# Linear attention: the first layer's opening steps moved into the last cycles of the cross attention before it

## The chip, the cores and the metric

One core of a Trainium2 chip runs the whole program in one launch. The metric is the device time of that launch in microseconds (us). The engines named below are TensorE (PE, with its weight loads as PEld), VectorE (DVE), ScalarE (ACT), GpSimd (POOL), and SyncE (SP), whose queue issues most of the DMAs. They run side by side, each through its own list of instructions in order, and wait for each other by semaphores.

## The reference, cut to what matters

The model is a stack of cross attentions, self attentions and feed-forward layers over 16 sequences of 64 tokens with 256 features, so 1024 tokens. Only its first two blocks bear on the change. The first is a cross attention of 16 heads against a context of 1601 rows for each of the 16 sequences, whose output is added to `x`:

```
scores = einsum('bhqd,bhkd->bhqk', qp, kp) / sqrt(d_k)   # masked where exactly 0 in the lower triangle
x = x + concat(softmax(scores) @ vp) @ w_o
```

The second is a linear attention of four layers. Its input is a layer norm of `x` times sqrt(256) with a table of positions added, and each layer begins with a layer norm of its own:

```
y = (x - mean) / sqrt(var + 1e-5) * sqrt(D) + pos        # once, the input of layer 0
h = (y - mean) / sqrt(var + 1e-5) * ln1_s + ln1_b        # each layer
q, k, v = h @ Wq + bq, h @ Wk + bk, h @ Wv + bv          # elu(q)+1, elu(k)+1 follow
y = y + (linear attention of q, k, v) @ Wo + bo
y = y + relu(norm(y) @ W1 + b1) @ W2 + b2
```

After the four layers a final norm of `y`, scaled by `lnf_s` and shifted by `lnf_b`, is added to `x`, and a mixture of experts follows.

## The kernel before, in words

Tokens lie on the 128 partitions in eight tiles of 128 (`self.x[:, t]`, two sequences each), all in float32.

The cross attention (`l0_xattn`, L201) is a stream over 16 sequences of 13 context chunks of 128 rows. `stream` (L341) writes its order out by hand for PE: each cycle makes the scores of two chunks by matmuls into one PSUM tile of four banks (`sc`, one buffer), ACT takes their exponential (`e`, L327, three buffers), PE multiplies `e` with the values (`acc`), and POOL adds `e` into the running sums of the softmax (`tot`, L2385). For the last sequence POOL sums only the chunks below 7; PE does the others in `add_sums` (L2285). In the last cycles, where there is nothing left to project, `out(t)` (L336) multiplies token tile t's heads with `wo` and DVE adds the result to `x` (L358). At the end `finish(xs[B - 1])` runs `finish_heads` (L2293): the last sums on PE, then on DVE a reciprocal (`rec`), two products (`half`) and their sum into `xT`, and then `out(7)` makes the last token tile. PE's instructions are pinned to the order of the text (`self.mm`, `self.tr`); those of DVE, ACT and POOL here are put in order by a scheduler.

The linear attention (`l0_attn`, L414) works on two halves of four token tiles, `a` and `b`, with its tiles in a pool on the other side of the memory (`l0a`). Tiles there lie over tiles of the cross attention, and an instruction that first writes one waits for the last reader of what lay below. Before the first layer, `measure` (statistics by bn_stats and bn_aggr, a square root on ACT), `start` (subtract the mean on ACT, multiply and add the positions on DVE) and `norm` (subtract and multiply on DVE) are done for both pairs of tiles of half `a` and the first pair of `b`; the second pair of `b` follows inside the projections of `a`. All of this stands behind the cross attention. `project` (L538) is a generator: `turn` transposes two token tiles on PE and evacuates them with the norm's scale and shift, `kv(t)` projects keys and values of a token tile and DVE evacuates them, `exp_keys` and `larger` make elu+1 of the keys on ACT and DVE, and the queries follow feature by feature. `go(pr, n)` runs n steps of it. In this function V, A and G are DVE, ACT and POOL pinned to the order of the text.

`self.row` (L96) loads a row of biases and spreads it over the partitions. `row_L_attn_bk.0` (L101) holds layer 0's bk, bv, bo and b2, of which DVE needs the first two to evacuate keys and values.

Of the kernel before, what the change touches and what calls it, by code (L numbers as in the profile page):

```python
# [12 lines left out]
F32 = mybir.dt.float32  # L13
I32 = mybir.dt.int32
BF16 = mybir.dt.bfloat16
AF = mybir.ActivationFunctionType
ALU = mybir.AluOpType
# [3 lines left out]
P = 128  # L21
# [43 lines left out]
class Sections:  # L65
# [135 lines left out]
    def l0_xattn(self):  # L201
        nc, tc, d = self.nc, self.tc, self.d

        self.held = ExitStack()
        self.routed = self.held.enter_context(tc.tile_pool(name="l0r", bufs=1, reuse_waits="tile"))
        with ExitStack() as ctx:
            sb = ctx.enter_context(tc.tile_pool(name="l0x", bufs=1, reuse_waits="tile"))
            sb2 = ctx.enter_context(tc.tile_pool(name="l0x2", bufs=2, reuse_waits="tile"))
# [119 lines left out]
                return e  # L328

            def finish(x):  # L330
                self.finish_heads(sb2, hT, x.b, x.acc, self.sums_of(x), ones)

            def extra(x):
                return [(maxima, x, g, i) for g in range(2) for i in range(3)] + [(last_maxima, x), (max_rows, x)]
# [1 line left out]
            def out(t):  # L336
                pm = ps.tile([P, D], F32, tag="bk", name="lin", padded_shape=[P, 512])
                for k in range(KC):
                    self.mm(pm, hT[:, k, t * P : (t + 1) * P], wo[:, k, :], start=(k == 0), stop=(k == KC - 1))
                self.add_to_x(t, pm)  # L340

            self.stream(ps, sb2, load, wk, wv, copy, weights, finish, out, extra)

# [70 lines left out]
    def l0_attn(self):  # L414
# [5 lines left out]
        for name, shape, dt in (("logits", [P, NT, E], F32), ("count", [P, NT + 1, E], F32), ("wt", [P, NT, 2], F32), ("hot", [P, NT, 2, E], F32),  # L420
# [8 lines left out]

        self.taken = tc.dram_tile([E * CAP + 2 * T, D], F32, name="taken")  # L430
        self.given = tc.dram_tile([E * CAP, D], F32, name="given")
        zero = pool.tile([P, D], F32, tag="zero", name="zero")
        nc.gpsimd.memset(zero, 0.0)
        nc.sync.dma_start(
            self.taken[: E * CAP].rearrange("(j p) d -> p j d", p=P), zero.unsqueeze(1).to_broadcast([P, E * CAP // P, D]))
        nc.gpsimd.memset(to.count[:, 0], 0.0)
        views = dram_disjoint_views(self.taken, 2 * NT)
        with ExitStack() as ctx:
# [10 lines left out]

            mask = self.c("mask136")  # L450
            pos = self.c("pos")
            lnf = self.row(sb, "L0_attn_lnf_s", "L0_attn_lnf_b")

            class Half:

# [21 lines left out]
                A.activation(r, r, AF.Sqrt)  # L477
                s.by[p] = mv, r

            def norm(s, src, p):  # L480

                mv, r = s.by[p]
                V.reciprocal(r, r)
                for j in range(2):
                    t = 2 * p + j
                    V.tensor_scalar(s.n[:, t, :], src[:, t, :], mv[:, j, 0:1], r[:, j : j + 1], ALU.subtract, ALU.mult)
# [15 lines left out]
            def add_row(s, r):  # L502
                G.tensor_tensor(s.y, s.y, r.unsqueeze(1).to_broadcast([P, HT, D]), ALU.add)
# [11 lines left out]
                    self.mm(pm, xT[:, k, t * P : (t + 1) * P], w[:, k, :], start=(k == 0), stop=(k == kc - 1))  # L515
                return pm

            def weights(l):
                w = lambda: None
                w.wq = self.w2(d["L0_attn_Wq"][l], "wq")  # L520
                w.wkv = self.wp.tile([P, KC, 2 * D], F32, tag="w8", name="wkv", bufs=3, padded_shape=[P, KC, 1024])
                for j, k in enumerate(("L0_attn_Wk", "L0_attn_Wv")):
                    nc.sync.dma_start(w.wkv[:, :, j * D : (j + 1) * D], d[k][l].rearrange("(c p) n -> p c n", p=P))
                w.wo = self.w2(d["L0_attn_Wo"][l], "wo")
                w.w1 = self.w8(d["L0_attn_W1"][l], "w1")
                w.w2 = self.w8(d["L0_attn_W2"][l], "w2")
                rows = self.row(sb2, *(f"L0_attn_{k}.{l}" for k in ("bk", "bv", "bo", "b2")))
                w.bk, w.bv, w.bo, w.b2 = (rows[:, i * D : (i + 1) * D] for i in range(4))
                for k in ("bq", "b1", "ln1_s", "ln1_b", "ln2_s", "ln2_b"):
                    setattr(w, k, self.v(f"L0_attn_{k}.{l}"))  # L530

                w.bq1 = sb2.tile([P, KC], F32, tag="bq1", name="bq1")
                w.bk1 = sb2.tile([P, D], F32, tag="bk1", name="bk1")
                for out, of in ((w.bq1, w.bq), (w.bk1, w.bk)):
                    G.tensor_scalar(out, of, 1.0, 0.0, ALU.add, ALU.add)
                return w

            def project(s, w):  # L538

                def kv(t):
                    pm = by_token(w.wkv, t, s.hT)
                    V.tensor_tensor(s.kz[:, t, :], pm[:, 0:D], w.bk1, ALU.add)
                    V.tensor_tensor(
                        s.va[:, t, :, 0:128], pm[:, D : 2 * D].rearrange("p (g x) -> p g x", g=2),
                        w.bv.rearrange("p (g x) -> p g x", g=2), ALU.add)

                def two(t):
                    return (a[:, t : t + 2, :].rearrange("p t x -> p (t x)") for a in (s.kz, s.tmp))  # L550

                def exp_keys(t):
                    z, e = two(t)
                    A.activation(e, z, AF.Exp, bias=less)

                def larger(z, e):
                    V.scalar_tensor_tensor(z, e, 1.0, z, ALU.min, ALU.max)

                qe = [s.h1T[:, c, :] for c in range(KC)]
                turn(s, 0, w.ln1_s, w.ln1_b)  # L560
                yield
                for t in range(2):
                    kv(t)
                    yield
                turn(s, 1, w.ln1_s, w.ln1_b)
                add_row(s, w.bo)
                exp_keys(0)
                yield
                for c in range(KC):
                    pm = by_feature(w.wq, c, s.hT)  # L570
                    A.activation(qe[c], pm, AF.Exp, bias=w.bq[:, c : c + 1])
                    A.activation(s.qT[:, c, :], pm, AF.Identity, bias=w.bq1[:, c : c + 1])
                    larger(*(two(0) if c == 0 else (s.qT[:, 0, :], qe[0])))
                    yield
                kv(2)
                larger(s.qT[:, 1, :], qe[1])
                yield
                kv(3)
                yield
                exp_keys(2)  # L580
                larger(*two(2))

            def attend(s, w):

# [96 lines left out]

            def start(s, p):

                mv, r = s.by[p]
                less = sb.tile([P, 2], F32, tag=f"less{s.i}", name="less", bufs=2)
                V.tensor_scalar(less, mv[:, :, 0], -1.0, 0.0, ALU.mult, ALU.add)
                V.reciprocal(r, r)
                V.tensor_scalar(r, r, math.sqrt(D), 0.0, ALU.mult, ALU.add)
                for j in range(2):
                    t = 2 * p + j  # L690
                    A.activation(s.n[:, t, :], s.x[:, t, :], AF.Identity, bias=less[:, j : j + 1])
                    V.scalar_tensor_tensor(s.y[:, t, :], s.n[:, t, :], r[:, j : j + 1], pos, ALU.mult, ALU.add)

            def mix(at, fd):

# [95 lines left out]
            nc.gpsimd.memset(less, -1.0)  # L791
            self.pinned = True
            a, b = Half(0), Half(1)

            a.make("h1T")
            b.make("h1T", "tmp")
            a.make("tmp", "hT", "kz", "va", "qT")
            b.make("n", "kz", "va", "hT", "qT", "y")
            a.make("y", "n")
            w = weights(0)  # L800

            V.pinned = False
            for s, n in ((a, 2), (b, 1)):
                for p in range(n):
                    measure(s, s.x, p)
            for s, n in ((a, 2), (b, 1)):
                for p in range(n):
                    start(s, p)
                    measure(s, s.y, p)
                for p in range(n):  # L810
                    norm(s, s.y, p)
            V.pinned = True
            for s in (a, b):
                nc.gpsimd.memset(s.va[:, :, :, 128:136], 1.0)
            pr = project(a, w)
            go(pr, 3)
            measure(b, b.x, 1)
            go(pr, 1)
            start(b, 1)
            measure(b, b.y, 1)  # L820
            go(pr, 1)
            norm(b, b.y, 1)
            go(pr)
            for s in (a, b):
                G.tensor_tensor(s.x, s.x, lnf[:, D:].unsqueeze(1).to_broadcast([P, HT, D]), ALU.add)
            at, pr = attend(a, w), project(b, w)
            go(pr, 4)
            for _ in range(4):
# [4 lines left out]
            at, fd = attend(b, w), feed(a, w)  # L833
            go(fd, 2)
            mix(at, fd)
            for l in range(1, 4):
                w0, w = w, weights(l)
                for s, ws, o, wo in ((a, w, b, w0), (b, w, a, w)):
# [27 lines left out]
            go(route(b, 1))  # L866
            squares(999)
            self.pinned = False

    def weighted_experts(self, ps, sb2, xT, comb, n, hidden, down):  # L870

# [1418 lines left out]
                    acc[32 * j : 32 * j + 32, 2 + g, :], self.c("ones")[:w, :32], weights[g][j], start=False, stop=True,  # L2290
                    skip_group_check=True)

    def finish_heads(self, sb2, hT, b, acc, totals, ones, eps=None):  # L2293


        nc = self.nc
        self.add_sums(acc, totals, P)
        rec = sb2.tile([P, 2, P], F32, tag="rec", name="rec")
        if eps is None:
            nc.vector.reciprocal(rec, acc[:, 2:4, :])  # L2300
# [21 lines left out]
    def scores_by_key(self, pm, pair, stop):  # L2322
# [3 lines left out]
        for h, (x, c) in enumerate(pair):  # L2326
            i = min(c // 4, 2)
            a = (c - 4 * i) * P
            for g in range(2):
                for r in range(4):  # L2330
# [3 lines left out]
                        x.qb[o, g].rearrange("p h s -> p (h s)"),  # L2334
                        start=(h == 0 and g == 0), stop=stop, skip_group_check=True,
                    )

    def sums_of(self, x):
        return [[x.tot[:, j, 2 * g : 2 * g + 2, :].rearrange("p h s -> p (h s)") for j in range(4)] for g in range(2)]
# [481 lines left out]
```

## Time and profile before

| | us |
|---|---|
| median of 3 runs (3752.28 to 3766.32) | 3760.18 |
| the profiled execution | 3753.96 |
| its span in the profile | 3752.2 |
| PE busy in the span | 3440.3 (92%) |
| DVE, ACT, POOL busy | 1974.1, 1451.3, 1291.0 |
| 850 to 860 us: PE, DVE, ACT busy | 10.00, 2.40, 5.04 |
| 860 to 870 us: PE, DVE, ACT busy | 1.75, 8.70, 2.00 |
| 870 to 880 us: PE, DVE, ACT busy | 1.38, 9.32, 1.61 |
| 880 to 890 us: PE, DVE, ACT busy | 7.46, 3.79, 2.05 |
| 890 to 900 us: PE, DVE, ACT busy | 5.19, 6.73, 7.22 |

The profile is one execution on the chip. A line of the timeline gives the start in us, the duration in us, the engine, the line of the kernel, the operation, what it writes and reads, its shape, how many instructions were merged, and in brackets how long the engine sat idle before it and who ended that. A line of the chain of waits gives start, duration and what held the end of the program up at that time. Where a helper class issues the instruction, its line is L59 (V, A and G), and for pinned matmuls and transposes it is L2452 and L2457. The cross attention ends at about 860 us of the span, the linear attention at about 1359 us.

### The profile page before, as it was taken

The numbers are of one execution on the slowest core, as the hardware profiler recorded it, in microseconds if no ns is written. First come the engines' busy times: TensorE is split into PE (matmuls) and PEld (weight loads), VectorE is DVE, ScalarE is ACT, GpSimd is POOL, SyncE is SP. The second block draws the span as 40 slices with busy tenths as digits, with TensorE's granted clock in tenths as the row PEclk, the third lists the DMA queues.
The fourth block names the chain that finished last, engine by engine and source line by source line (L and its number), as shares of the span: only waits on it lengthen the run. The fifth ranks groups of instructions, "written<-read, shape, count | busy, mean of one in ns | idle before, by whom it ended". The sixth has DMA issues, their size and how long they took to land.

```text
span 3752.2 us, 70803 instructions
## 1 busy us (share of the span) xinstructions
PE 3440.3 (92%) x30966; PEld 2187.8 (58%) x30966; DVE 1974.1 (53%) x3676; ACT 1451.3 (39%) x2076; POOL 1291.0 (34%) x787
## 2 busy tenths in 40 slices
PE   8999999996999969999977988999999789999986
PEld 4555555563665645555545666667767555555554
DVE  5344333436555546656657554577767665333346
ACT  2333333333444414444423443466666612111213
POOL 1555555562011123333321001577777630000012
PEclk9999999998999979999989999999999989999997
DMA  4111001101332344343101001111111004111640
GB/s 145 38 38 38 31 27 38 38 10 35 105 96 87 111 158 163 127 146 110 37 26 40 1 6 44 68 56 38 56 38 38 11 2 174 43 36 30 278 180 13
DMA packets 106123, 258.66 MB, mean 69 GB/s; under 512 B 9203, under 2 KB 74483, under 8 KB 103510
## 3 DMA queue, kind: packets, MB, share of 16 engines
q1 hardware_dynamic: 97366, 222.68, 16.6%
q10 hardware_dynamic: 6912, 27.27, 2.3%
q8 instruction: 243, 3.98, 0.4%
q0 software_dynamic: 1536, 4.20, 0.4%
q14 instruction: 66, 0.54, 0.0%
HBM read 248.34 MB, written 5.77 MB: 68 GB/s over the span
## 4 chain that ended last, share of the span: by engine, by line
PE 77%; DVE 12%; ACT 7%; issue 2%; DMA 1%; POOL 1%; SPq 0%; ACTq 0%; DVEq 0%; POOLq 0%
PE sc L2452 15%; PE pk L2452 15%; PE lin L2452 7%; PE acc L2452 6%; PE lin_t L2452 5%; ACT e L327 5%; PE pu L2452 4%; PE lin L194 3%; PE gate L2017 3%; PE up L2017 3%; PE pc L1639 3%; PE prz L2452 2%; PE gelu_t L1549 2%; PE turn L2457 2%; PE pa L2452 1%
## 5 line engine op out<-in xcount | busy, mean ns | idle before, releaser
L2385 POOL TENSOR_TENSOR tot<-tot,e 128x1024 f32<-128x1024 f32 (+1 forms) x340 | 802.9, 2361 | 374.5 <-ACT e L327 251.2
L270 DVE TENSOR_REDUCE m<-sc 128x4 f32<-128x2048 f32 x96 | 220.1, 2293 | 271.3 <-PE sc L2452 270.2
L1779 DVE SCALAR_TENSOR_TENSOR e<-sc,row_L_xattn_nbias,free 128x2048 f32<-128x2048 f32 x104 | 244.3, 2349 | 121.8 <-PE sc L2452 116.3
L1781 ACT ACTIVATE e<-e 128x2048 f32<-128x2048 f32 x104 | 198.7, 1910 | 243.2 <-DVE e L1779 243.2
L327 ACT ACTIVATE e<-sc 128x2048 f32<-128x2048 f32 x104 | 195.2, 1877 | 241.2 <-PE sc L2452 239.6
L2452 PE MATMUL sc<-qb,kT 32*128 32x128 f32 x6656 | 244.8, 283 | 36.6 <-DVE m L284 12.3
L2452 PEld LDWEIGHTS sc<-qb,kT 32*128 32x128 f32 x6656 | 205.9, 187 | 80.6 <-issue 24.5
L2452 PE MATMUL acc<-e,v 128*32 128x128 f32 x6656 | 226.6, 276 | 6.4 <-ACT e L1782 6.4
L2452 PEld LDWEIGHTS acc<-e,v 128*32 128x32 f32 x6656 | 170.3, 110 | 105.7 <-issue 95.1
L2452 PE MATMUL pk<-cT,wk 128*128 128x512 f32 (+1 forms) x512 | 207.0, 534 | 3.6 <-DVE rows L300 3.6
L2452 PE MATMUL pk<-wv,cT 128*128 128x256 f32 x832 | 209.8, 394 | 0.0
L1782 ACT ACTIVATE e<-e 128x2048 f32<-128x2048 f32 x104 | 198.7, 1911 | 3.3
L2452 PE MATMUL pk<-cT,wkv 128*128 128x512 f32 (+1 forms) x512 | 197.2, 526 | 0.0
L2452 PE MATMUL pk<-wkv,cT 128*128 128x256 f32 x832 | 196.3, 386 | 0.0
L2452 PEld LDWEIGHTS pk<-wv,cT 128*128 128x128 f32 x832 | 149.7, 190 | 75.5 <-issue 58.2
L2452 PEld LDWEIGHTS pk<-wkv,cT 128*128 128x128 f32 x832 | 153.3, 190 | 28.3 <-issue 4.3
L1639 PE MATMUL pc<-ew,eh 128*128 128x256 f32 x640 | 158.8, 391 | 0.0
L2452 PE MATMUL pu<-cn,e 128*64 128x257 f32 (+1 forms) x1248 | 146.5, 391 | 12.9 <-POOL e L1186 12.9
L2452 PE MATMUL sc<-kT,qb 32*128 32x512 f32 (+2 forms) x1536 | 140.8, 465 | 14.9 <-DVE m L270 2.3
L2021 ACT ACTIVATE g<-gate 128x512 f32<-128x512 f32 x68 | 40.6, 597 | 292.2 <-PE gate L2017 292.2
L1176 POOL TENSOR_TENSOR e<-e,mx 128x512 f32<-128x512 f32 x96 | 81.8, 883 | 194.7 <-DVE mx L1175 194.7
L2022 DVE TENSOR_TENSOR hT<-up,g 128x512 f32<-128x512 f32 x68 | 47.0, 692 | 178.8 <-PE up L2017 174.6
(519 smaller groups left out, 6339.5 us busy)
## 6 DMA issues: line engine op xcount, KB each, us to landing
cT<-in_ctx_t SPq DMA_DIRECT2D x128, 832.0 KB, 6.1
cn<-in_ctx_n SPq DMA_DIRECT2D x32, 1664.0 KB, 12.6
piece<-in_ctx_n ACTq DMA_DIRECT2D x32, 640.0 KB, 3.9
w<-in_L_attn_W SPq DMA_DIRECT2D x8, 1024.0 KB, 7.2
piece<-in_ctx_n ACTq DMA_DIRECT2D x16, 384.0 KB, 3.5
w<-in_L_ffn_W SPq DMA_DIRECT2D x16, 256.0 KB, 4.8
down<-in_L_ffn_w_down SPq DMA_DIRECT2D x16, 256.0 KB, 2.7
gate<-in_L_ffn_w_gate SPq DMA_DIRECT2D x16, 256.0 KB, 2.7
```

The source lines that it names most:

```text
L194: nc.tensor.matmul(pm, xT[:, k, t * P : (t + 1) * P], w[:, k, :], start=(k == 0), stop=(k == kc - 1))
L270: nc.vector.tensor_reduce(x.m4[:, g, :, i], pm, AX.X, ALU.max)
L327: nc.scalar.activation(e, pm, AF.Exp, scale=0.25)
L1176: pin(nc.gpsimd.tensor_tensor(p.e, p.e, p.mx.unsqueeze(2).to_broadcast(p.shape), ALU.subtract))
L1549: nc.tensor.matmul(pm, w[:, c, lo : lo + m], cT[:, c, :], start=(c == 0), stop=(c == nk - 1))
L1639: nc.tensor.matmul(pc[:, n, j, :], s.eh[i][:, c, tok], ew2[:, c, cols], start=False, stop=(c == 3))
L1779: nc.vector.scalar_tensor_tensor(e16, pm16, nb, free[:, at : at + P].unsqueeze(1).to_broadcast([P, 16, P]), ALU.add, ALU.mult)
L1781: nc.scalar.activation(e, e, AF.Relu)
L1782: nc.scalar.activation(e, e, AF.Square)
L2017: nc.tensor.matmul(pm[-1], w[:, k, n * P : (n + 1) * P], xT[:, k, tok], start=(k == 0), stop=(k == KC - 1))
L2385: nc.gpsimd.tensor_tensor(tot[:w], x.first if c == 1 else tot[:w], e[:w], ALU.add)
L2452: ins = self.nc.tensor.matmul(*args, **kw)
```

## The change

In `l0_xattn` a new pool `l0y` is opened below the cross attention's own pools and kept to the end of `l0_attn`. It holds half `a`'s `y` and `hT`, and small tiles for the statistics. `out(t)` now also measures the token tile, takes roots after tiles 3, 5 and 7, and for half `a` makes `y` (after tiles 4 and 5) and its norm (after 5 and 6); the transposes of half `a` stand inside the last `finish_heads`, between the last sums on PE and the reciprocal on DVE. Roots there are made as exp(-ln(v)/2) on ACT with one Newton step on DVE.

```
+        self.begun = self.begin(self.at_once.enter_context(tc.tile_pool(name="l0y", bufs=1, reuse_waits="tile")))
...
+                self.finish_heads(sb2, hT, x.b, x.acc, self.sums_of(x), ones, between=turned if x.b == B - 1 else None)
...
+            def start(t):
+                if t == 0:
+                    nx.n = sb2.tile([P, KC, SKP], F32, tag="cT", name="n")[:, 0, : 4 * D].rearrange("p (t d) -> p t d", d=D)
+                nc.scalar.activation(nx.n[:, t], self.x[:, t, :], AF.Identity, bias=nx.less[:, t : t + 1])
+                nc.vector.scalar_tensor_tensor(nx.y[:, t, :], nx.n[:, t], nx.r[:, t : t + 1], pos, ALU.mult, ALU.add)
+                nx.measure(nx.y[:, t, :], nx.mvy[:, t])
+            def norm(p):
+                two = slice(2 * p, 2 * p + 2)
+                nx.root(nx.ry[:, two], nx.mvy[:, two], 1.0)
+                for t in range(2 * p, 2 * p + 2):
+                    nc.vector.tensor_scalar(
+                        nx.n[:, t], nx.y[:, t, :], nx.mvy[:, t, 0:1], nx.ry[:, t : t + 1], ALU.subtract, ALU.mult)
+            def turned():
+                for p in range(2):
+                    pt = ps.tile([P, KC, 2, P], F32, tag="bk", name="tr")
...
+                            self.tr(pt[:, c, j, :], nx.n[:, 2 * p + j, c * P : (c + 1) * P], self.ident)
+                    for c in range(KC):
+                        nc.scalar.activation(
+                            nx.hT[:, c, 2 * p * P : (2 * p + 2) * P], pt[:, c].rearrange("p j x -> p (j x)"), AF.Identity,
+                            bias=ln_b[:, c : c + 1], scale=ln_s[:, c : c + 1])
...
                 self.add_to_x(t, pm)
+                nx.measure(self.x[:, t, :], nx.mv[:, t])
+                if t in (3, 5, 7):
+                    nx.roots(0 if t == 3 else t - 1, t + 1)
+                if t in (4, 5):
+                    start(2 * (t - 4))
+                    start(2 * (t - 4) + 1)
+                if t in (5, 6):
+                    norm(t - 5)
...
+        def root(r, mv, scale, V=nc.vector, A=nc.scalar):
+            vq = pool.tile([P, 2, 4], F32, tag="vq", name="vq")
+            v, q = vq[:, 0, : r.shape[1]], vq[:, 1, : r.shape[1]]
+            V.tensor_scalar(v, mv[:, :, 1], 1e-5, 1.0 / scale**2, ALU.add, ALU.mult)
+            A.activation(q, v, AF.Ln)
+            A.activation(r, q, AF.Exp, scale=-0.5)
+            V.tensor_tensor(q, r, r, ALU.mult)
+            V.scalar_tensor_tensor(q, v, -0.5, q, ALU.mult, ALU.mult)
+            V.scalar_tensor_tensor(r, q, 1.5, r, ALU.add, ALU.mult)
+        def roots(lo, hi):
+            root(nx.r[:, lo:hi], nx.mv[:, lo:hi], math.sqrt(D))
+            nc.vector.tensor_scalar(nx.less[:, lo:hi], nx.mv[:, lo:hi, 0], -1.0, 0.0, ALU.mult, ALU.add)
```

In `l0_attn` the projections of `a` start from the finished `hT` (`project(a, w, True)` skips both `turn`s and puts `add_row` at its end), and both pairs of `b` are prepared between their steps, with roots by `root` on V and A. The row of biases of layer 0 is loaded into `l0a` early in the order of its tiles, and the addition of `lnf_b` to `x` is put behind the first mix of attention and feed-forward. The tile of zeros that clears `taken` in memory is half as wide and is written by two DMAs:

```
-            a.make("h1T")
-            b.make("h1T", "tmp")
...
+            a.y, a.hT = nx.y, nx.hT
+            a.make("n", "tmp", "qT")
+            b.make("y")
+            rows0 = weights_rows(0)
+            a.make("kz", "va")
+            b.make("n", "hT")
+            a.make("h1T")
+            lnf = self.row(sb, "L0_attn_lnf_s", "L0_attn_lnf_b")
+            b.make("tmp", "kz", "va", "qT", "h1T")
+            w = weights(0, rows0)
...
-            pr = project(a, w)
-            go(pr, 3)
-            measure(b, b.x, 1)
-            go(pr, 1)
-            start(b, 1)
...
+            pr = project(a, w, True)
+            go(pr, 1)
+            start(b, 0)
+            go(pr, 2)
+            norm(b, b.y, 0, True)
+            start(b, 1)
+            go(pr, 2)
+            norm(b, b.y, 1, True)
             go(pr)
-            for s in (a, b):
-                G.tensor_tensor(s.x, s.x, lnf[:, D:].unsqueeze(1).to_broadcast([P, HT, D]), ALU.add)
...
-        zero = pool.tile([P, D], F32, tag="zero", name="zero")
+        zero = pool.tile([P, P], F32, tag="zero", name="zero")
...
+        for k in range(KC):
+            nc.sync.dma_start(
+                self.taken[: E * CAP, k * P : (k + 1) * P].rearrange("(j p) d -> p j d", p=P),
+                zero.unsqueeze(1).to_broadcast([P, E * CAP // P, P]))
```

## The prediction

> **What bounds the kernel now.** First the page's shares: PE is busy 92% of the span and the chain that ended last lies on PE for 77%. So only a stretch where PE stands idle can give time. The busy time by 10 us shows one at the seam between the cross attention and the linear attention: PE is busy 10.00 of 10 until 860, then 1.75, 1.38, 7.46 and 5.19. There I read the chain of waits:
>
> ```profile
> 856.35 4.12 PE acc L2452 x144
> 860.48 1.77 DVE rec L2300
> ...
> 863.26 1.35 PE lin L2452 x4
> 864.64 0.42 DVE x L358
> ...
> 873.59 2.87 DVE y L59 x2
> ...
> 880.40 5.75 PE lin L2452 x8
> ...
> 891.73 3.07 DVE y L59 x2
> ...
> 898.95 3.80 PE lin L2452 x4
> ...
> 905.27 5.26 PE lin L2452 x8
> ```
>
> From 860.46 to 880.40 the end waits for DVE: the last heads, then statistics, roots, `y` and `n` of three pairs of tiles. A second, smaller hole lies inside the projections of half a (the second pair of b, 891.7 to 898.95). The `lin` at 880.40 is a's first kv, the one at 905.27 is b's; they are 24.87 apart. I call their starts R and Q. After Q the work is the same, so the change's gain is the move of Q, less what it costs elsewhere.
>
> Two things in the timeline decide how early the moved work can run. DVE and POOL:
>
> ```profile
> 841.36 12.16 POOL L2385 TENSOR_TENSOR tot<-tot,e 128x1024 f32<-128x1024 f32 x5
> ...
> 848.76 2.45 DVE L2311 TENSOR_TENSOR xT<-half 128x128 f32<-128x128 f32 x1
> ...
> 855.41 1.88 ACT L327 ACTIVATE e<-sc 128x2048 f32<-128x2048 f32 x1 [2.38 <-PE sc L2452]
> ...
> 862.92 0.29 DVE L2311 TENSOR_TENSOR xT<-half 128x128 f32<-128x128 f32 x1
> ...
> 877.38 1.31 DVE L59 TENSOR_SCALAR ln_r<-ln_mv 128x2 f32<-128x2 f32 x1
> ```
>
> The same sum into xT takes 0.29 when POOL is still and 2.45 while POOL adds; a tiny scalar step takes 1.31 (0.17 elsewhere) until POOL's addition ends. DVE steps that read PSUM (x at 841.40, 0.42) and bn_stats (0.74 for two beside POOL) do not stretch. So until POOL's last sum at 853.5 each root step on DVE waits up to 2.43. And ACT:
>
> ```profile
> 2093.53 1.06 ACT L1649 ACTIVATE sp<-sp 128x1024 f32<-128x1024 f32 x1
> 2094.49 0.58 ACT L1643 ACTIVATE g<-pc 128x512 f32<-128x512 f32 x1
> 2095.09 1.28 ACT L1650 ACT_TABLE_LOAD   x1
> 2096.38 1.06 ACT L1650 ACTIVATE sp<-sp 128x1024 f32<-128x1024 f32 x1
> ```
>
> This is another block, the only one with ln: L1649 is an exp, L1650 a ln. All 12 ln of the trace come with a table load of 1.28, though the set before them served exp. No row has an exp straight after a ln; bounds 0 and 1.28. I take 1.28, since whoever placed these loads never chose a set that would serve both. So a root costs 2 loads and 2 steps of 0.20: 2.96 on ACT. The root by sqrt that it replaces also costs a load there and one back (892.11, 896.33).
>
> The Trainium skill ("ScalarE: Activation LUTs", Table sets: the hidden batching unit) says that ln followed by exp needs one load, since one set has both. By that rule the later roots would be free of loads and, by the steps below, the time some 7 us lower. The 12 rows speak against it.
>
> **Step 1: a's norm in the tail.** x3 is added at 844.85 and ready at 845.27. Measure: 0.39 + 0.18, so 845.85. The first root (tiles 0 to 3): its scalar step waits for POOL's addition until 846.2; ln and exp with their loads fill ACT from the end of `e` (845.73) to 848.7. The next `e` could start at 847.70, so it is late by 1.0. Three DVE steps and `less` (0.7 by themselves) wait at 851.1 and 853.5 for POOL: ready near 854. Bounds: 850 (no waiting), 856 (a wait at every step). Then four subtractions on ACT (0.45 each), on DVE four y and measures (4 x (0.44 + 0.57) = 4.0) and tiles 4 to 6 added and measured (3 x 0.99 = 3.0): DVE is done with y near 861. It also has rec, half and xT, 2.7 from 860.5 on.
>
> On ACT three more roots are due (tiles 4 and 5, the two pairs of y): 3 x 2.96 = 8.9. The last `e` ends at 857.3, with the delay 858.3. If all come after it, they end at 867; if the lns are batched or run before it, at 861. I take 865 for the last n. To it: n 0.73 (872.86), transposes 0.66 (8 of 16; the others are earlier), and `out(7)`, which PE's pinned order puts between transposes and kv: 1.35. ACT evacuates hT beside it (2 x 0.56). **R becomes 869** with the tail's delay of about 1; range 864 to 876.
>
> The other conditions for R: wkv was issued at 19.85, long before. layer 0's row of biases was issued at 864.67, when out(7) had read xT below it, and POOL had it at 868.72. In the new order of tiles it comes, by their sizes, over the values of sequence 14, whose last matmul is at 837.85; even at the old time it lands before the first evacuation, R + 3.9. `bk1` on POOL (1.09) now waits for out(7), also ready in time.
>
> **Step 2: from R to Q.** Pinned order, in us after R. kv0 reaches its evacuation after 3.9 (880.40 to 884.29, clock granted 0.77 there); evacuation 0.76: 4.7. b's first pair: y 0.89, measures 1.2, scalar step 0.2, ln 0.2, load 1.28, exp 0.2, three steps 0.65: 9.4. The root of tiles 6 and 7 (2.96 on ACT, after out(7)) fits before it. kv1's evacuation 0.76, n 0.73: 10.9. The second pair likewise, 4.6: 15.5; DVE then does `larger` 0.69. ACT frees the queries' first PSUM buffer at 16.4 (exp and identity, 0.57 each in a row), which kv(3) waits for, because `mm` has three; after 4 us idle it takes 3.8 as at 898.95: 20.2. Evacuation 0.76, exp_keys 0.72, larger 0.69, hT 0.46: 22.9. b's `add_row` on POOL (2.34) starts when n has been read and holds `larger` up by 1.4: **Q is R + 24.3**, against 24.87 now. Two y stalls of over 2 us go (POOL's x additions at 876.15 and 892.17 are gone from here), two roots behind kv's evacuation come in their place.
>
> **Sum.** Q: 869 + 24.3 = 893.3 against 905.27, so -12.0.
>
> **Edits at nothing.** (a) The lnf_b additions, 2 x 2.5 on POOL, fall in the first mix, where PE is busy 10.00 of 10 (940 to 960) and POOL idle; DVE, 3.79 to 4.57 of 10, may wait 2.5 once or twice, three PSUM buffers of 1.9 cover that: 0 to +2. (b) The zeros in two DMAs: SP issued the one at 13.17, one more issue is 0.38. The DMA engines are full until 35, while the chain is DVE's gate biases until 33.33 and the next DMA is issued at 55.55; all of it twice is 1280 KB at 370 GB/s = 3.5: 0, bounds 0 and +3.5. (c) Seven measures in the tail, 0.57 each: DVE is busy 0.85 to 4.46 of 10 there. (d) lnf_s is loaded later, needed at 1290. (e) The 16 transposes, 0.15 to 0.17 each, run beside rec (1.77), where PE stood idle: 0; if n is late, they are in R already. (f) POOL's sums wait for DVE's short steps: 5 x 0.2 = 1, in the delay above.
>
> **The rivals.** *More is gained:* lns batched, or one set for both; R at 864, two loads fewer before Q, kv0 at full clock (0.43 for 0.86, 8 matmuls less 2): -19, between -17 and -22. For it: the scheduler can pair waiting lns. Against: the 12 loads. *Half is given back:* the roots queue one after the other behind the last `e` and POOL's waits come at every step: R at 875, -6. *The work does not move ahead:* now every DVE step of this kind stands behind the last xT (863.13); if the list puts the new ones there too, six steps of y and roots follow it as now: R near 880, 0. Against: they are in the same function now, and x was ready from 834.9. *Slower:* ACT runs in order. If ln or the subtractions are listed ahead of `e` at 851.14 and 855.41, `e` waits for DVE, which waits for POOL: each up to 2.45 + 2 x 1.28 = 5.0, PE's end 10 later, at 870.5, then the roots of 8.9, n, transposes and out(7): R at 882.5 and Q at 906.8, +1.5; with (a) and (b) above at their upper ends +7. It decides from R = 881 on. For it: PE has nothing else to do between `sc` and `e` but one `acc` and `lin`; against: `e` stands first in the text and ACT is idle for 1.57 to 2.38 before each.
>
> **How the numbers follow.** The profiled execution took 3753.96 (span 3752.2), 6.2 below the median 3760.18 of the runs shown. -12.0 gives 3742 for such a one and 3748 against the median, which I forecast. Chances: forecast (-8 to -16) 0.53, more 0.19, half 0.14, not ahead 0.06, slower 0.08. 0.5% is 18.8, about what a measurement of this kernel can tell from no change. Faster by more: nearly all of "more" that passes it, 0.15, and 0.02 from the runs' own spread of 14. Slower by more: only if the slower case's stalls come to more than twice their price, or by something that I have not seen: 0.05. Within: 0.78. The range takes -22 of the faster case to the edge of "not ahead" and +2: 3738 to 3762.
>
> **What would show it.** Right: `rec` within 2 us of 860.5; the first `lin` of attention near 869; two table loads at each root; transposes and hT's evacuation beside `rec`; no y of 3 us; Q near 893; the rest moved by the same amount. Wrong: table loads missing; an `e` that waits for DVE or ACT for over 2 us; R after 876; an interval from R to Q above 28; a difference after Q, in the mix or at the experts, of over 3 us.

## The result, and the profile after

The changed kernel takes 3759.37 us, the kernel before on the same chip 3755.47 (medians of 13 runs each). The ratio, which is estimated from all the runs and is not the quotient of the two medians, is 1.0001, with a 95% interval from 0.9991 to 1.0010: no measurable difference, where 12 us less were forecast. The profiled execution took 3760.83 (span 3758.7).

To see where the time went I matched each instruction of DVE, ACT and POOL with its counterpart in the kernel before and took the difference of their starts. It is +1.8 by 80 us and stays so until 838; from 920 to 1340 it is a constant -3.5. So the seam gained 5.3, not 12. Behind it the difference rises to +6.6: by 0.9 between 1350 and 1375, by 5.1 near 1412 and by 5.5 between 3058 and 3080, the rest in smaller steps. The two large steps are not the seam's: e4 below, which has nothing of the work at the seam, has 4.5 and 5.6 at the same places. Below, "net" means less the difference at 765, ahead of the seam.

The chain of waits through the seam (start, duration, what):

```profile
850.98 1.87 DVE vq L2407
...
853.11 2.16 DVE vq L2408
...
855.86 1.58 DVE y L344 x4
...
860.96 1.28 ACT L2406
862.26 0.20 ACT r L2406
862.48 1.28 ACT L2405
...
863.99 1.28 ACT L2406
...
868.90 0.20 ACT ry L2406
869.11 1.77 ACT e L329
870.92 4.54 PE acc L2532 x80
875.49 1.77 DVE rec L2348
...
878.37 1.11 PE lin L2532 x4
```

Before, this stretch was PE's last sums, `rec` at 860.48 and then 20 us of DVE. Now the chain runs over table loads on ACT, and it still has to pass the last `e`. ACT's own rows in the timeline show what stands ahead of it:

```profile
852.05 1.85 ACT L329 ACTIVATE e<-sc 128x2048 f32<-128x2048 f32 x1
856.58 1.88 ACT L329 ACTIVATE e<-sc 128x2048 f32<-128x2048 f32 x1 [2.67 <-PE sc L2532]
858.47 1.28 ACT L2405 ACT_TABLE_LOAD   x1
860.74 0.20 ACT L2405 ACTIVATE vq<-vq 128x2 f32<-128x2 f32 x1 [0.98 <-DVE vq L2404]
...
867.61 1.28 ACT L2406 ACT_TABLE_LOAD   x1
868.90 0.20 ACT L2406 ACTIVATE ry<-vq 128x2 f32<-128x2 f32 x1
869.01 1.86 ACT L329 ACTIVATE e<-sc 128x2048 f32<-128x2048 f32 x1
```

The scores of that last `e` were complete at 862.66:

```profile
862.27 0.39 PE L2532 MATMUL sc<-rows,minus 32*128 32x512 bf16 x4
```

ACT takes its work in order, and three roots with six loads were listed ahead of it; two of the three waited for DVE as well (0.98 ahead of the ln at 860.74, 0.60 ahead of the one at 867.39). So `e` starts 6.35 late. The `e` at 852.05 is late too, by 2.7, behind the first root's exp load and the subtractions. PE waits, and the clock falls (window, its length, busy time of PE, PEld, DVE, ACT, POOL, then the granted clock):

```profile
860.00:870.00 10.00, 5.61 (x144) 4.41 (x136) 4.34 (x22) 8.53 (x12) 1.57 (x5) 0.98 0.01 2
870.00:880.00 10.00, 8.03 (x94) 6.56 (x95) 4.53 (x11) 4.09 (x6) 2.36 (x1) 0.66 0.36 128
```

From `rec` on the change does what it was to do: the transposes and the evacuation of hT run beside it, and a's first kv product starts 3.8 behind it (19.9 before). It starts at R = 879.30, b's at Q = 901.91: net 2.9 and 5.2 earlier than before.

Then the experts. The queue of SP in the kernel before:

```profile
1331.71 0.41 SPq L101 DMA_DIRECT2D row_L_ffn_b<-in_rows  x1
1332.22 12.29 SPq L914 DMA_DIRECT2D w<-in_L_ffn_W  x8
```

and after the change:

```profile
1328.23 0.34 SPq L101 DMA_DIRECT2D row_L_ffn_b<-in_rows  x1
1348.21 4.11 SPq L960 DMA_DIRECT2D w<-in_L_ffn_W  x8
```

Eight weight loads of 256 KB, whose tiles the diff does not touch, go out 20 us later behind the row of biases, just as ACT's last step on a `piece` of the context (1348.00, 0.19) ends. From 1350 to 1360 the DMA engines are then busy 0.93 and 0.75 of each 5 us (0.00 and 0.22 before), and the scatter into `taken`, which everything waits for there, takes longer (before, then after):

```profile
1358.90 2.39 DMA taken<-n,put
```

```profile
1355.40 4.37 DMA taken<-n,put
```

### The profile page after: what moved, and what is told of

It is laid out like the page before. It is cut to its first block, busy times and chain, and to the rows that moved or that the text cites. A ratio compares the mean times of both kernels' runs of the same rounds, so it can differ in the third digit from the quotient of the medians.

```text
span 3758.7 us, 70806 instructions
## 1 busy us (share of the span) xinstructions
PE 3441.4 (92%) x30951; PEld 2185.7 (58%) x30966; DVE 1971.7 (52%) x3681; ACT 1466.3 (39%) x2094; POOL 1292.2 (34%) x787
## 4 chain that ended last, share of the span: by engine, by line
PE 76%; DVE 13%; ACT 8%; issue 2%; DMA 1%; POOL 0%; another core or an unknown queue 0%; SPq 0%; ACTq 0%; DVEq 0%; POOLq 0%
PE sc L2532 15%; PE pk L2532 15%; PE lin L2532 6%; PE acc L2532 6%; PE lin_t L2532 5%; ACT e L329 5%; PE pu L2532 4%; PE lin L194 3%; PE gate L2063 3%; PE up L2063 3%; PE pc L1685 3%; PE prz L2532 2%; PE gelu_t L1595 2%; PE turn L2537 2%; PE pn L2532 1%
## 5 line engine op out<-in xcount | busy, mean ns | idle before, releaser
L2532 PE MATMUL sc<-cT,qT 128*64 128x512 f32 (+1 forms) x768 | 141.9, 522 | 3.8 <-ACT scs L1202 3.3
```

The lines of the kernel that those rows point to most:

```text
L2532: ins = self.nc.tensor.matmul(*args, **kw)
```

## The experiments

Theory: the gain at the seam is eaten because ACT's roots, with their loads, are listed ahead of `e`; the later loss is the late weight loads. Rivals: POOL's sums, which hold DVE's small steps; the loads as such, wherever they stand; the clock's accidents. Q is given net (905.27 before, 900.1 after the change).

**e1_dve_roots**: no root on ACT. In `root`:

```diff
-A.activation(q, v, AF.Ln)
-A.activation(r, q, AF.Exp, scale=-0.5)
+near = D if scale == 1.0 else 1.0 / D
+V.tensor_scalar(r, v, -0.5 * near**-1.5, 1.5 * near**-0.5, ALU.mult, ALU.add)
+for _ in range(2 if scale == 1.0 else 3):
     V.tensor_tensor(q, r, r, ALU.mult)
...
```

The loop holds the three lines of the Newton step. The variance of y is near 256 by construction; that of x is near 1 in these data, and this root of x holds only near there.

> The changed kernel with every root of the new pool taken by VectorE alone: a tangent at the nominal variance (256 of y, 1 of x) and two or three steps of Newton instead of Ln, Exp and one step. No table load and no root on ScalarE is left in the tail, all else is as in the changed kernel. Theory (ScalarE works in order, and the roots with their loads are listed ahead of e): the last e starts within 2 us of 860 instead of 869.0, rec near 864 instead of 875.5, a's first kv product (R) at 867 to 870 instead of 879.3, b's (Q) at 889 to 892 instead of 901.9; 9 to 12 us less than the changed kernel, 0.997 of it. Rival (VectorE's small steps wait for POOL's sums, and so y and the roots are late whoever takes them): the last e is early too, but n is ready as late as now, R stays at 876 or later, and no more than 3 us are gained.

The three last `e` start at 848.78, 852.48 and 856.46, each within 0.4 of the end of its scores. Q = 892.6, a gain of 12.7 instead of 5.2. The time is 0.9984 of before (0.9975 to 0.9993). So the roots on ACT, their loads and their place in the order together, cost 7.5 of the gain. R (873.30) was later than expected, and `rec` came at 868.62 although PE's last sum ended at 863.0: DVE is the bound now. Its column, the third after the window's length:

```profile
850.00:860.00 10.00, 8.32 (x205) 6.39 (x198) 9.68 (x24) 4.39 (x3) 4.30 (x2) 1.00 0.01 2
860.00:870.00 10.00, 5.07 (x120) 3.91 (x111) 8.98 (x42) 1.79 (x4) 3.77 (x6) 0.79 0.38 133
```

**e2_e_first**: the loads stay, the order changes.

```diff
-if t in (3, 5, 7): nx.roots(0 if t == 3 else t - 1, t + 1)
+if t in (3, 7):    nx.roots(t - 3, t + 1)
-if t in (5, 6):    norm(t - 5)
 def turned():
+    nc.vector.tensor_scalar(eps, nx.e[:, 3, 511:512], 0.0, 1e-5, ALU.mult, ALU.add)
+    norm(0, eps)
+    norm(1, eps)
...
```

> The changed kernel with the two roots of a's norm put behind the last e: their 1e-5 comes out of a VectorE step that reads the last e, and the root of tiles 4 and 5 is taken together with that of 6 and 7. Ln, Exp and their table loads remain (two fewer loads). Theory (the order on ScalarE is what costs): the last e starts near 860, rec near 864, the two roots take 2 x 3.5 us behind the last e, so n at 869 and R at 872 to 874; 5 to 8 us less than the changed kernel. Rival (the loads cost wherever they stand, the order does not matter): R within 2 us of 879.3, and no gain.

The rows of ACT:

```profile
860.31 1.88 ACT L329 ACTIVATE e<-sc 128x2048 f32<-128x2048 f32 x1 [2.73 <-PE sc L2536]
862.21 1.28 ACT L2409 ACT_TABLE_LOAD   x1
...
868.45 1.00 ACT L367 ACTIVATE hT<-tr,vecs 128x256 f32<-128x256 f32 x2
```

The last `e` waits for PE alone, R = 874.53 (expected 872 to 874), Q = 896.3; 0.9979 of before (0.9967 to 0.9991). Q is 3.9 earlier than in the changed kernel. One root with its two loads is gone too, 3.0 on ACT, so the order by itself is worth between 0.9 and 3.9; the rival that the order does not matter (R within 2 us of 879.3) falls. `rec` was later than expected (869.8): DVE's root steps stand ahead of it.

**e3_short_pool**: `if x.b < B - 1 or c < 7` becomes `c < 3` for POOL's sums.

> The changed kernel with POOL's sums of the last sequence cut from seven chunks to three; TensorE adds the other four as it adds the last six now. So VectorE's small steps in the tail do not wait for POOL. Ln, Exp, their loads and their place among the e remain. Theory (the order on ScalarE): the last e still stands behind the roots and their loads, R at 876 or later. Rival (POOL's sums hold VectorE, and so the roots, back): the y's start 4 to 6 us earlier, the last e as well, R at 872 to 874.

R = 877.32, and the last `e` at 867.03 still stands behind six loads. Q = 897.9, 2.3 earlier than the changed kernel's. Both effects exist; the roots on ACT are the greater one (7.5 in e1), as the theory had it. One run, 3757.86.

**e4_zero_only**: the kernel before with the two transfers of zeros.

> The kernel before with one edit of the change alone: the zeros go out in two transfers of half a row, from a tile half as wide. If these two transfers cause the 1.8 us that the changed kernel is behind at 78, this kernel is behind by 1.5 to 2.0 there too, and the granted clock falls to 0.50 near 71. If that step comes from the clock alone, which can fall at the same place in any run, the start is within 0.6 us of the kernel before up to 838, or is behind by another amount.

0.3 behind from 80 to 838 (3755.13, one run). The granted clock did fall for one stretch near 68, and still the start was not 1.8 late: in this run the transfers did not bring that step.

**e5_right** and **e6_dve_right**: `tile_pool(name="l0y", bufs=1, side="right")` in the changed kernel and in e1.

> The changed kernel with its new pool laid at the other end of SBUF, where the pool of the linear attention lies too, and nothing else. Theory (the eight weight loads of the expert layer write where y and hT of half a still lie, and so wait for the end of the linear attention): their issue falls from 1348.2 to within 2 us of the row of L0_ffn_b2, near 1328; the scatter into taken then takes near 2.4 us instead of 4.5 and 1.5 to 3.5 us of the changed kernel's time go. The seam itself stays as it is, R near 879. Rival (that loss comes from where the clock's windows fall): the loads move or not, and the time stays within 1 us.

> e1_dve_roots with the new pool at the other end of SBUF. Theory: the two gains add up, since they lie in two places: R near 873, weight loads issued near 1320, and 8 to 11 us less than the kernel before (0.997 to 0.9978 of it). Rival (what the seam gains is given back at the expert layer whatever the loads do, by a wait on something that is not moved): no more than the 6 us that e1_dve_roots gained.

The theory of *where* the loads collide failed: they are issued at 1344.6, 20 us behind the row as before, and the scatter takes 4.68. So it is not a's y and hT that they wait for. Q = 899.8 and 892.6, as without the edit. 0.9989 (0.9975 to 1.0002) and 0.9982 (0.9971 to 0.9993) of before.

**e7_fewer_short** and **e8_fewer_roots**: e6 with one root for the four tiles of y; the last two lines, POOL's sums, in e7 alone.

```diff
-if t in (3, 5, 7): nx.roots(0 if t == 3 else t - 1, t + 1)
+if t in (3, 7):    nx.roots(t - 3, t + 1)
-if t in (5, 6):    norm(t - 5)
+if t == 6:         norm()
...
-if x.b < B - 1 or c < 7:
+if x.b < B - 1 or c < 3:
```

> e6_dve_right with VectorE's work in the tail cut: one root for all four tiles of y instead of two, the root of tiles 4 and 5 taken with that of 6 and 7, and POOL's sums of the last sequence cut from seven chunks to three. Theory (with ScalarE free, VectorE is the bound of the tail: from 849.6 it waits for POOL and from 854.4 it works without a gap to 871.3): R at 865 to 868 instead of 873.3, 5 to 8 us less than e6_dve_right. Rival (TensorE is next: it takes four more sums, its last sum ended at 863.0 already): R not below 871.

> e7_fewer_short with POOL's seven sums kept. Theory (19 small steps of 0.2 us are gone from VectorE ahead of rec and n): R at 868.5 to 870.5; what is between it and e7_fewer_short is the price of POOL's sums, 2 to 4 us. Rival (POOL's sums cost nothing here, since TensorE ends after them): R within 1 us of e7_fewer_short.

Q = 889.4 in e8 and 886.1 in e7 (R 869.26 and 866.59). So 3.2 lay in the 19 small steps and 3.3 in POOL's sums. That is the rival of e3, dearer (3.3 against 2.3) once ACT is out of the way. e7: 0.9974 (0.9962 to 0.9986); e8, one run: 3744.11.

**e9_weights_low**: in the expert layer of the changed kernel the tiles of these weights come first.

```diff
+late = [sb.tile([P, 2, KC, D], F32, tag=f"w{e}", name="w12") for e in range(E // 2, E)]
 b2w = sb.tile([P, 2, D], F32, tag="b2w", name="b2w")
...
-both = sb.tile([P, 2, KC, D], F32, tag=f"w{e}", name="w12")
+both = late[e - E // 2]
```

> The changed kernel with one edit in the expert layer: its four tiles w12 for the weights of experts 4 to 7 are laid down before xs, xw, ys, yw and xsT instead of after them. Theory (in the changed kernel w12 lies where the squares of the context write until 1348.0, and the weight loads wait for that): the loads are issued right behind the row of L0_ffn_b2, near 1328, the scatter into taken takes 2 to 3 us instead of 4.5, and 1.5 to 3 us that the changed kernel loses between 1350 and 1375 are kept; the seam is as in the changed kernel. Rival (that loss has another cause): the loads are early and the loss between 1350 and 1375 stays as it is.

```profile
1327.10 0.34 SPq L101 DMA_DIRECT2D row_L_ffn_b<-in_rows  x1
1327.50 6.19 SPq L961 DMA_DIRECT2D w<-in_L_ffn_W  x8
```

```profile
1354.65 2.40 DMA taken<-n,put
```

The difference to the kernel before is -4.3 at 1345 and -4.6 at 1390: nothing is lost. The eight kernels with late loads lose 0.8 to 2.5 there, the changed kernel the least, and have scatters of 4.07 to 5.00; the five with early loads (e4, e9, e10, e11 and the second profile of before) gain 0.4 to 0.9 on the first profile of before and have scatters of 2.40 to 2.56. So the late loads cost 1.2 to 3.4, 2.5 between the two means; in the changed kernel's own profile it is 1.2 to 1.7. What they waited for was the memory under `w12`: it lies over what the squares of the context use until 1348, probably because the change made the linear attention's pool smaller and reordered it. That reason is inferred from the time at which they go; that the place of the tiles decides is shown. Whole time: 0.9991 (0.9981 to 1.0002).

**e10_all**: e7 without `side="right"`, with e9's edit.

> e7_fewer_short, but the new pool where the change put it, and the four weight tiles first as in e9_weights_low: every cause found so far taken away. Theory: R at 865 to 868, 18 us ahead of the kernel before at 1340 by the trace and still 17 or more behind the expert layer at 1375; 0.9965 to 0.9975 of the kernel before. Rival (part of any gain at the seam is given back at the expert layer): the lead falls by 2 or more between 1340 and 1375, as it does in all the other kernels with the change.

```profile
857.88 4.12 PE acc L2533 x144
862.02 1.77 DVE rec L2348
...
864.89 1.12 PE lin L2533 x4
```

R = 865.83, Q = 886.1; -18.5 at 1340 and -19.3 at 1390. 3744.91 against 3759.91, a ratio of 0.9964 (0.9951 to 0.9976). The interval lies below 1, and below that of the changed kernel (0.9991 to 1.0010). `rec` is back beside its place before the change, with the norm done by then.

**b2_before_again**: no edit.

> The kernel before once more, for a second profile of it. If the steps by which the profiled executions differ far behind the seam (at 1400, 2040 and 3040) belong to single executions, this profile differs from the first by steps of up to 6 us there too, with no edit between them. If they belong to the change, the two profiles agree within 1 us from end to end.

3749.56. Between the two profiles of one program there are steps of -1.4 near 945, +2 near 1412, -2 near 1920 and -2 to -3 near 3680. In e9, which is the changed kernel there, +5.3 come at 1970, where the chain has 3.25 of "issue", and none in the changed kernel's own profile. The step of 5.5 or more at 3060 stands in eleven profiles, that of e4 among them, and not in the two of before and that of e10, which has all of the change's work at the seam; in the changed kernel the granted clock there is 0.55 from 3060 to 3070 (0.95 before). So steps of that size behind 1400 say nothing of the change at the seam. What decides them stays open. At the seam the profiles repeat: Q is 899.8 in e5 and in e9, whose seam is the changed kernel's (900.1), and 905.4 and 905.3 in this profile and e4's (905.27), so the rival that the clock's accidents made the loss there falls.

**e11_x_by_ln**: e10 with the roots of x by Ln and Exp again, so that only the root of y relies on its known variance.

> e10_all, but the roots of x (whose variance depends on the data) go by Ln and Exp on ScalarE again, as in the change; only the roots of y, whose variance the norm before holds near 256, are VectorE's tangent and two Newton steps. Two roots of x are left, that of tiles 0 to 3 ahead of three e's and that of 4 to 7 behind the last. Theory (a root listed ahead of e costs its two loads there, one behind the last e nothing until b's part): the e behind the first root is late by 2 to 3 us, the last e is late by 1 to 3 against e10_all's 856.9, R at 867 to 870 instead of 865.8; 0.997 to 0.998 of the kernel before. Rival (the loads now fit into the time in which ScalarE is idle): R within 1 us of e10_all.

The `e` behind the first root starts at 851.16, the last at 858.76; R = 867.73, Q = 887.4, 1.3 behind e10. 0.9969 (0.9957 to 0.9982). The first of these `e` is 1.8 later than its scores. Net, R is 0.8 behind e10, within what the rival allowed, so the cost is there and smaller than expected; this version does not depend on the variance of x.

## Where the prediction was right and where it was wrong, point by point

The time lies in the range, and no measurable difference was the likeliest case. That is in part luck: the range, 3738 to 3762, holds the forecast of 3748 as well as no gain at all, and so does not tell the two apart. The 12 us that carried the forecast did not come. Seven of them were lost at the seam, by one step of the prediction; a smaller part was lost at the experts. Two of its own signs of being wrong came: an `e` late by more than 2 us, and R after 876.

- **What bounds the kernel: right.** Eight of the eleven kernels that shortened the seam have at 1340 what they had at Q, within 0.8; e2, e3 and e5 have 1.7 to 3.3 more there, and 1.4 more come without any work at the seam (e4 and the second profile of before).
- **The price of a root: right.** All ten ln and exp at L2405 and L2406 carry a load of 1.283, exp straight behind ln too, where no row had existed. The Trainium skill ("ScalarE: Activation LUTs", Table sets: the hidden batching unit) has one set with both; in this program's traces no root of the change was served by it.
- **DVE under POOL's sums: right.** The root was expected near 854 and y done near 861: r ended at 855.6, the last measure of y at 861.3 (net 853.8 and 859.5).
- **The step that failed** is in step 1: "If all come after it, they end at 867; if the lns are batched or run before it, at 861. I take 865 for the last n." They ran before it, and not for nothing. The three roots held ACT, with two waits for DVE, from 858.47 to 869.01, and the last `e` behind them started 6.35 late. The step asked when the roots would be done and not what stands behind them in ACT's order. R came at 877.5 net, not 869.
- **The rival "slower" had this mechanism in part** (chance 0.08): roots listed ahead of `e` on ACT. It counted one root for each `e` where three stood ahead of the last, and so sized the parts too low: each `e` up to 5.0 late (2.7 and 6.35), PE's end 10 later (`rec` is 13.2 later net). Its R of 882.5 was too late all the same, by adding the 8.9 of roots behind PE's end a second time: roots that stand ahead of `e` are done by then. With R at 877.5 there is still a gain.
- **Step 2**: R to Q 24.3 expected, 22.6 measured; 20.1 with no root on ACT (e1, e10). The addition of b's row on POOL held up DVE's `qT` at 897.04 (2.45) and not `larger` behind kv(3) (0.69), so the 1.4 that it was to cost there did not come. The clock of 0.77 that is given for kv0 is the mean from 880 to 890; while kv0 ran it was 0.50.
- **The sum.** -12.0 at Q is about what the tail gives when no root is left on ACT: -12.7 in e1, -19.2 when DVE and POOL are relieved too. From the changed kernel to e10 that is 7.5 (ACT's order and loads), 3.2 (DVE's steps) and 3.3 (POOL's sums).
- **Edits at nothing.** (a) and (d) right: the difference stays -3.5 from 920 through the mix and to 1340. (b) Right: 0.3 in e4. (c) The seven measures were not tested by themselves; with no root on ACT, DVE is the bound (9.68 and 8.98 of 10 in e1), and 19 other short steps there cost 3.2. (e) Right: the transposes ran beside `rec`. (f) Priced at 1 and not seen: the five sums took 12.10 (12.16 before).
- **What was not seen**: "the rest moved by the same amount". The text followed the queues that the diff names, and not the memory. Eight weight loads far behind the seam went out late, and of the 5.3 that the changed kernel's profile is ahead at 1340 it has 4.4 at 1390; over all profiles late loads cost 2.5 in the mean.
- **The trace and the median.** Net, the changed kernel's profile is 4.4 ahead of the first profile of before at 1390 and 2.5 ahead of the second; the interval of the ratio is -3.4 to +3.8 us. For e10 it is 19.1 and 17.3, and the interval 9.0 to 18.4 (13.5). In the same way the nine kernels that have an interval fall short of the first profile by 0.7 to 7.5, and of the second by up to 5.6. Where this goes stays open: the profiles of single executions differ behind 1400 by steps as large.

## What to carry to other kernels

When work is moved into a gap of an in-order engine, ask what stands behind it in that engine's list, not only when the moved work is done: a step that waits for another engine makes the pacemaker wait. Take the next engine into the sum at once, since relieving ACT here showed DVE, and relieving DVE showed POOL. After an edit of pools, compare the issue times of every transfer far behind the edit, because the tiles that they write may lie over something else than before.

## What the runs showed of the hardware

The granted clock falls to 0.50 in stretches that are multiples of 3.4 us (3.41, 6.83, 10.24, 13.65, 20.48 and longer ones) in all fourteen profiles, but for the last stretch of each, which lies over the program's end. Where they lie decides small differences. The windows of the changed kernel near 70, against 1.00 throughout before:

```profile
68.00:70.00 2.00, 2.00 (x29) 1.27 (x23) 0.00 (x0) 0.17 (x1) 0.00 (x0) 0.65 0.03 8
70.00:72.00 2.00, 2.00 (x3) 0.88 (x3) 0.00 (x0) 1.71 (x1) 0.21 (x1) 0.50 0.00 0
```

Both kernels leave PE idle for 2.81 us just ahead of this. In the changed kernel's profile the clock then halves for 3.4 us, four matmuls into `pk` take 3.10 instead of 1.98, and most of the +1.8 at the start comes from there. In the other profiles of kernels with the change the start is between -0.2 and +2.1 off, and the second profile of before has a stretch at 66.5 too, so the fall is no property of the change. The Trainium skill ("TensorE: Matmul & The Clock Gate", What's actually happening) speaks of a free-running window of 3413 ns; the length agrees, and that the page's windows do not start with the program would explain why they fall differently in each execution, which no run here tests.

In six of the fourteen profiles, with the change and without, ACT's first `scs` of the next cross attention waits 5.1 to 6.4 us for something that the trace does not name (6.36 in the changed kernel's, 5.74 in e4's, none in the first profile of before). It was not settled.
